# A one-core conv, FFT and FFN kernel: x waits in DRAM for the inverse, the nonlinearity's parts get tiles of their own, ScalarE sums x, and the planner gets margins

## The chip, the cores and the metric

The kernel runs on one core of a Trainium2 chip. The metric is device time in microseconds of one launch. The median of three runs before the change is 4435.95 us (4433.51 to 4437.45). Engine names are those of the profile: PE is TensorE (PEld its weight loads), DVE is VectorE, ACT is ScalarE, POOL is GpSimd, and SP is SyncE, whose queue issues nearly all DMAs.

## The reference, cut to what matters

The input is 32 images of 56 x 56 pixels and 96 channels in float32. Each image passes two layers.

```python
# layer 0: a mixture of 4 experts, weighted per image
pooled = jnp.mean(x, axis=(1, 2));  rw = sigmoid(pooled @ Wr + br)
h = relu(bn1(x @ mix(rw, Wpw) + rw @ bpw))            # 96 -> 384 channels
h = relu(bn2(sum_i rw_i * (depthwise3x3(h, Wdw_i) + bdw_i)))
x = bn3(h @ mix(rw, Wpwl) + rw @ bpwl) + x            # 384 -> 96, "x1" in the kernel
# layer 1, over the image's 3136 tokens t
h = relu(bn(layernorm(t) @ w1.T))                     # 96 -> 192
X = fft(h, tokens)
xr = relu(X.real*rd - X.imag*idg + rb);  xi = relu(X.imag*rd + X.real*idg + ib)
t = t + bn(ifft(xr + 1j*xi).real @ w2.T)
t = t + ffn(layernorm(t))                             # fp8 operands, 96 -> 384 -> 96
```

The pooled mean needs the whole image before the first matrix product of layer 0; the FFT needs all tokens of an image before any frequency, and the inverse needs all frequencies before any token.

## The kernel before, in words

Tokens lie along the free axis and channels on the partitions. x of an image lives in one of three SBUF buffers (`xpad`, line 326); it is loaded there, the projection adds to it in place, the inverse adds to it, the FFN adds to it, and strips of a quarter image are written out from it. So image b can only be loaded when image b-3 is out (`loads`, line 566).

The work of one image is cut into stages, each a Python generator ("stream"). `mixing` (573) sums x on DVE (`pooled`), mixes the expert weights (`wk`, `small`, `wk2`) and copies `wk2` to shifted partitions with six DMAs. `expansion` (643) is the product 96 -> 384 into `ps_pw`, evacuated by ACT to `hp`. The depthwise convolution is split: `convolved_tensor` (678) does four 32-channel blocks at once on PE in three waves of 288 matmul passes (`ps_dw`), and `convolved_vector` (722) does the rest on DVE in steps of one tap. `projection` (748) gives `ps_pwl`, and `projected` (770) adds it to x on DVE. `forward` (814) does layernorm moments by transposes (`ps_t_a`), the product with w1 (`ps_w1`, shown as `ps_w`), the first DFT step (`ps_a`), and sends the result to DRAM (`gd`). `frequency_loads` and `frequencies` bring it back transposed (`g2`), do the second DFT step (`ps_b`), and spawn `nonlinearity` (889) and `spectrum` (934), which does w2 and the first inverse step (`ps_w2`, `ps_c`) and sends `zo` to DRAM (`yd`). `inverse` (979) loads quarter strips `yt`, does the last inverse step (`ps_d`), adds it to x on DVE, transposes again (`ps_t_f`), and runs the FFN (`ps_n`, `ps_f1`, `ps_f2`); POOL casts the hidden values to fp8 and does the last addition before the strip goes out.

The order of all instructions on all engines is written by a planner (`Plan`, 131) when the program is built. It holds a clock per engine, a duration formula per operation (`Engine`, 242, and `mm`, 547), a count of free PSUM tiles (four) and of a few SBUF tiles, and due times of DMAs (`arrives`, 560). `Plan.run` (199) always takes the stream that can start first; ties go by priority. Each engine runs its instructions in exactly that order, and waits at any whose data are not there. Where the planner sees PE wait, `psum` (317) puts in filler matmuls that compute nothing:

```python
for _ in range(min(40, int((plan.idle() - 0.3) / 0.19))):
    nc.tensor.matmul(ps[:PB, 0:PB], dftb_s, dftb_s, start=True, stop=True)
```

They are at line 321 and so can be told from real work (line 554, and 558 for transposes); most other instructions come from line 282.

Of the kernel before, what the change touches and what calls it, by code (L numbers as in the profile page):

```python
# [76 lines left out]
GK = 8  # L77
GROUPS = [(0, 16), (16, 13)]
# [52 lines left out]
class Plan:  # L131
# [9 lines left out]

    def __init__(self, **buffers):
        self.free = dict.fromkeys((PE, DVE, ACT, POOL, SP), 0.0)
        self.now = self.ready = 0.0
        self.events = {}
        self.streams = []

        self.buffers = {tag: [0.0] * n for tag, n in buffers.items()}
        self.busy = dict.fromkeys(self.free, 0.0)

        self.port = {DVE: (0.0, 0.0), POOL: (0.0, 0.0)}

        self.gap = (0.0, 0.0)
# [19 lines left out]
    def release_after(self, n, used):  # L173

        used.append(self.now)
        if len(used) == n:
            self.release(at=max(used))
# [21 lines left out]
    def run(self):  # L199
        while self.streams:  # L200
            best = None
            for stream in self.streams:
                if any(len(self.buffers[tag]) < n for tag, n in stream.takes.items()):
                    continue
                ready = stream.ready
                missing = False
                for key in stream.after:
                    at = self.events.get(key)
                    if at is None:
                        missing = True  # L210
                        break
                    ready = max(ready, at)
                if missing:
                    continue
                for tag, n in stream.takes.items():
                    ready = max(ready, self.buffers[tag][n - 1])
                key = (max(ready, self.free[stream.engine]), stream.priority, ready)
                if best is None or key < best[0]:
                    best = key, ready, stream
            if best is None:  # L220
                raise RuntimeError(
                    "no stream can go on: "
                    + "; ".join(
                        f"{s.name} {[k for k in s.after if k not in self.events]} {s.takes}"
                        for s in self.streams
                    )
                )
            _, ready, stream = best
            has = self.free[PE]
            for tag, n in stream.takes.items():  # L230
                has = max(has, self.buffers[tag][n - 1])
                del self.buffers[tag][:n]
            self.gap = (has, ready) if stream.engine == PE else (0.0, 0.0)
            self.now = self.ready = ready
            self._advance(stream)
# [6 lines left out]
class Engine:  # L242
# [12 lines left out]
    def __getattr__(self, name):  # L255
        def issue(out, *args, **kw):
# [24 lines left out]
            self.plan.tick(self.engine, us, port)  # L281
# [4 lines left out]
def kernel(  # L286
# [39 lines left out]
    xpad = [const([C, (S + 2) * S], F32, f"x_{i}") for i in range(min(3, NB))]  # L326
    xs = [xpad[b % 3][:, S : S + N] for b in range(NB)]
    for b in range(min(3, NB)):
        nc.gpsimd.memset(xpad[b][:, 0:S], 0.0)
        nc.gpsimd.memset(xpad[b][:, S + N :], 0.0)  # L330
# [209 lines left out]
    plan = Plan(ps=4, mir=2, zo=1, h16=4)  # L540
# [19 lines left out]
    def arrives(nbytes, *key):  # L560
        plan.done(*key, late=1.4 + nbytes / 220e3)

    mixed, small_of, wk2s, gds, yds, zs = {}, {}, {}, {}, {}, {}


    def loads():
        for b in range(NB):
            yield SP, [("out", b - 3, s) for s in range(NS) if b >= 3]
            if b:
                Q.dma_start(xs[b], x[b])  # L570
            arrives(4 * C * N if b else 0, "x", b)

    def mixing():

        for b in range(NB):
            yield DVE, [("x", b)] + [("x1", b - 2, s) for s in range(NS) if b >= 2]
            pooled = mixp.tile([C, 1], F32, tag="pooled", name=f"pooled_{b}")
            V.tensor_reduce(pooled, xs[b], AX.X, ALU.add)
            pool_b = mixp.tile([C, 128], F32, tag="pool_b", name=f"pool_b_{b}")
            V.behind.tensor_scalar(pool_b, ones, pooled, 1.0 / N, ALU.mult, ALU.mult)  # L580
# [25 lines left out]
            for c in range(NPE):  # L606
                plan.spawn("diagonals", 3, diagonals(b, c))
# [5 lines left out]
            yield SP  # L613

            wk2s[b] = [wk2]
            for q in range(1, G):
                wk2q = mixp.tile([128, NPE, C], F32, tag=f"wk2_{q}", name=f"wk2_{b}_{q}")
                for to, at in turned(q):
                    Q.dma_start(wk2q[to], wk2[at, 0:NPE])
                wk2s[b].append(wk2q)  # L620
# [22 lines left out]
    def expansion():  # L643

        for b, p, before in parts_of_all():
            xb = xpad[b % 3]
            for c in (2, 0, 1):

                for part, (at, ns) in enumerate((((0, (9, 9)), (18, (8, 8))), ((0, (8, 8)), (16, (9,))))[p]):
                    yield PE, [("wk", b)] + (readers(*before, c) if before else []), 1  # L650
                    wk = mixed[b]
                    ps = psum(f"ps_pw_{b}_{p}_{c}_{part}")
                    for j, n in enumerate(ns):
                        lo = (G * BW * p + at + j * n) * S
                        mm(
                            ps[:, 512 * j : 512 * j + n * S],
                            wk[:, 128 * c : 128 * c + 128],
                            xb[:, lo : lo + n * S],
                        )
                    plan.spawn("evac pw", 5, expanded(b, p, c, part, at, ns, ps))  # L660
# [17 lines left out]
    def convolved_tensor():  # L678

        for b, p, before in parts_of_all():  # L680
            for i, wave in enumerate(WAVES[p]):
# [24 lines left out]
                plan.spawn("evac dw", 0, convolved(b, p, i, wave, ps))  # L706
# [41 lines left out]
    def projection():  # L748

        for b, p, _ in parts_of_all():  # L750
            needs = [("h2t", b, p, i) for i in range(len(WAVES[p]))] + [("wk2", b)]
            needs += [("h2v", b, p, c) for c, *_ in ON_VECTOR[p]]
            for s, blocks in (((0, (0, 1)), (1, (2, 3))), ((2, (4, 5)), (3, (6,))))[p]:
# [13 lines left out]
                plan.spawn("evac prj", 3, projected(b, s, blocks, ps))  # L767
            plan.done("prj", b, p)

    def projected(b, s, blocks, ps):  # L770
# [8 lines left out]
        plan.done("x1", b, s)  # L779

# [33 lines left out]
    def forward(parity):  # L814

        for b in range(NB):
            for s in range(parity, NS, 2):
# [6 lines left out]
                for q0, nq in ((0, 4), (4, 3)):  # L824
                    yield PE, (), 1
                    ps = psum(f"ps_w1_{b}_{s}_{q0}")
                    for q in range(nq):
                        at = s * T + PB * (q0 + q)
                        mm(ps[:PB, 256 * q : 256 * q + CH], xt[:, at : at + PB], w1c)
                    yield DVE  # L830
# [39 lines left out]
    def frequencies():  # L870
# [4 lines left out]
        for b in range(NB):  # L875
            for i, (k0, nk) in enumerate(GROUPS):
                for kind in range(NKIND):
# [6 lines left out]
                    plan.spawn("nonlinearity", 3, nonlinearity(n, b, k0, size, kind, ps))  # L884
                plan.done("g2", n)
                plan.spawn("spectrum", 4, spectrum(n, b, i, k0, nk))
                n += 1

    def nonlinearity(n, b, k0, nk, kind, ps):
        rd, idg, rb, ib = (nl_s[:, j, kind : kind + 1] for j in range(4))  # L890
        nr = nrd[:, kind : kind + 1]
        re = slots(ps, 128, nk, 128, S)
        im = ps[:, 0 : nk * 128].rearrange("p (n w) -> p n w", w=128)[:, :, S:PB]
        yield ACT
        zt = sp.tile([128, GK, PB], F32, tag=f"z_{kind}", name=f"z_{b}_{k0}_{kind}")
        zs[n, kind] = zt
        zr, zi = zt[:, 0:nk, 0:S], zt[:, 0:nk, S:PB]
        A.activation(zi, re, AF.Identity, scale=idg, bias=ib)
        first = k0 == 0 and kind < 2
        if first:  # L900
            A.activation(zr, re, AF.Identity, scale=rd, bias=rb)
            yield DVE
            n0 = CH - 128 if kind else 128
            at0 = zt[:n0, 0, 0 : S + 1 : S]
            V.tensor_add(at0, at0, dc[:n0, kind, :])
        yield ACT, (), "mir"
        used = []
        m = sp.tile([128, GK, PB], F32, tag="mir", name=f"mir_{b}_{k0}_{kind}", bufs=2)
        mr, mi = m[:, 0:nk, 0:S], m[:, 0:nk, S:PB]
        plan.spawn("imaginary parts", 1, imaginary_parts(n, kind, im, zi, mi, rd, nr, used))  # L910
        if not first:
            A.activation(zr, re, AF.Identity, scale=rd, bias=rb)
# [5 lines left out]
        P.tensor_add(mr, mr, zr)  # L918
        yield ACT, [("im", n, kind)]
        A.activation(m[:, 0:nk, :], m[:, 0:nk, :], AF.Relu)  # L920
        yield DVE
        W.scalar_tensor_tensor(zr, zr, 2.0, mr, ALU.mult, ALU.max)
        W.scalar_tensor_tensor(zi, zi, 0.0, mi, ALU.max, ALU.subtract)
        plan.release("mir")
        plan.done("z", n, kind)

    def imaginary_parts(n, kind, im, zi, mi, rd, nr, used):
        yield DVE
        V.scalar_tensor_tensor(mi, im, nr, zi, ALU.mult, ALU.add)
        V.behind.scalar_tensor_tensor(zi, im, rd, zi, ALU.mult, ALU.add)  # L930
        plan.release_after(2, used)
        plan.done("im", n, kind)

    def spectrum(n, b, i, k0, nk):

        for at in range(0, nk, GK):
            some = min(GK, nk - at)
            needs = [("z", n, kind) for kind in range(NKIND)] + [("y", n - 1)] * (n >= 1)
# [40 lines left out]
    def inverse(parity):  # L979


        for b in range(NB):
            for s in range(parity, NS, 2):
                yield SP, [("yd", b, i) for i in range(len(GROUPS))]
# [4 lines left out]
                arrives(4 * PA * SQ * C, "yt", b, s)  # L989
# [6 lines left out]
                strip = xs[b][:, s * T : s * T + T]  # L996
# [8 lines left out]
                yield from moments(f"f_{b}_{s}", xs[b], s, f"f{parity}", got, nt)  # L1005
# [24 lines left out]
                for c in range(NC3):  # L1030
# [8 lines left out]
                    plan.spawn("hidden", 0, hidden(parity, b, s, c, ps, h8))  # L1039
# [22 lines left out]
                arrives(4 * C * T, "out", b, s)  # L1062
# [15 lines left out]
    with tc.manual_schedule():  # L1078
        for name, priority, stream in (
            ("loads", 0, loads()), ("mixing", 5, mixing()), ("inverse", 3, inverse(0)),  # L1080
            ("inverse", 0, inverse(1)), ("frequency loads", 4, frequency_loads()),
            ("frequencies", 3, frequencies()), ("forward", 2, forward(0)),
            ("forward", 1, forward(1)), ("projection", 7, projection()),
            ("vector", 8, convolved_vector()), ("tensor", 6, convolved_tensor()),
            ("expansion", 9, expansion()),
# [117 lines left out]
```

## Time and profile before

| what | value |
|---|---|
| median of three runs | 4435.95 us |
| the profiled execution | 4431.78 us, of which the span is 4429.7 us |
| busy: PE, DVE, ACT, POOL | 97%, 79%, 59%, 22% of the span |
| DMA | 339.19 MB, 16 engines busy 29% in mean |
| DMAs on SP's queue for one image | 41; 10.6 MB is the mean of all images |

The profiled execution was 4.2 us under the median, and 2.1 us of it lie outside the span. A f32 product counts as two matmul passes in the trace. The views used are: the page (busy shares, chain), groups of instructions (count, busy us, mean ns), waits (who waited for whom), the timeline (instructions in order of time, equal ones merged, with the idle time before them), and tables of busy time by stretch.

### The profile page before, as it was taken

The numbers are of one execution on the slowest core, as the hardware profiler recorded it, in microseconds if no ns is written. First come the engines' busy times: TensorE is split into PE (matmuls) and PEld (weight loads), VectorE is DVE, ScalarE is ACT, GpSimd is POOL, SyncE is SP. The second block draws the span as 40 slices with busy tenths as digits, with TensorE's granted clock in tenths as the row PEclk, the third lists the DMA queues.
The fourth block names the chain that finished last, engine by engine and source line by source line (L and its number), as shares of the span: only waits on it lengthen the run. The fifth ranks groups of instructions, "written<-read, shape, count | busy, mean of one in ns | idle before, by whom it ended". The sixth has DMA issues, their size and how long they took to land.

```text
span 4429.7 us, 114914 instructions
## 1 busy us (share of the span) xinstructions
PE 4278.0 (97%) x48916; PEld 3145.0 (71%) x48916; DVE 3503.1 (79%) x7222; ACT 2626.4 (59%) x4135; POOL 979.1 (22%) x1012
## 2 busy tenths in 40 slices
PE   6999999999999999999999999999999999999999
PEld 4767777777777677777677777677777677777778
DVE  6768878888877788877888787888788888788863
ACT  2455666665656655656655666556666656566654
POOL 1012222221222122222122222122222212222222
PEclk9999999999999999999999999999999999999999
DMA  3222233232333222332222332322332322332221
GB/s 92 59 71 63 74 93 81 71 81 67 77 93 80 70 75 71 81 90 74 78 75 71 82 84 72 87 70 71 87 84 71 87 69 67 92 80 71 80 72 50
DMA packets 305448, 339.19 MB, mean 77 GB/s; under 512 B 127908, under 2 KB 244452, under 8 KB 301636
## 3 DMA queue, kind: packets, MB, share of 16 engines
q1 hardware_dynamic: 302824, 331.70, 28.4%
q8 instruction: 384, 6.29, 0.6%
q14 instruction: 128, 1.05, 0.1%
q10 hardware_dynamic: 2112, 0.15, 0.0%
HBM read 164.06 MB, written 158.27 MB: 73 GB/s over the span
## 4 chain that ended last, share of the span: by engine, by line
PE 66%; DVE 15%; ACT 8%; DMA 7%; issue 3%; POOL 1%; SPq 0%; ACTq 0%; POOLq 0%; DVEq 0%
PE ps_dw L554 14%; PE ps_pwl L554 11%; PE ps_w L554 10%; PE ps_pw L554 7%; DVE h L282 6%; PE ps_a L554 5%; PE ps_b L554 4%; PE ps_f L554 4%; DMA x<-in_x_dram 4%; PE ps_c L554 2%; ACT z L282 2%; DMA yd<-zo 2%; DVE z L282 2%; ACT mir L282 2%; DVE pooled L282 2%
## 5 line engine op out<-in xcount | busy, mean ns | idle before, releaser
L282 DVE SCALAR_TENSOR_TENSOR h<-hp,small,h 128x1792 f32<-128x1792 f32 (+2 forms) x768 | 1292.6, 1683 | 33.0 <-ACT h L282 17.3
L554 PE MATMUL ps_dw<-hp,diag 32*32 32x448 f32 x27648 | 857.8, 544 | 9.9 <-issue 9.6
L554 PEld LDWEIGHTS ps_dw<-hp,diag 32*32 32x32 f32 x27648 | 537.9, 103 | 280.6 <-issue 95.8
L282 POOL CAST h<-h 128x784 fp8e5<-128x784 f16 x384 | 382.7, 1022 | 1183.8 <-DVE h L282 1183.8
L554 PE MATMUL ps_pw<-x,wk 96*128 96x448 f32 (+1 forms) x1344 | 572.3, 565 | 38.0 <-DVE z L282 33.8
L554 PE MATMUL ps_pwl<-h,wk 128*96 128x448 f32 x1344 | 526.3, 539 | 0.0
L282 ACT ACTIVATE hp<-ps_pw,small 128x896 f32<-128x896 f32 (+2 forms) x384 | 361.1, 953 | 270.0 <-PE ps_pw L554 256.0
L282 ACT ACTIVATE nt<-yt,nm,rstd_f 112x96 fp8e5<-112x96 f32 x896 | 334.5, 454 | 200.5 <-DVE nm L282 200.3
L554 PEld LDWEIGHTS ps_pw<-x,wk 96*128 96x128 f32 x1344 | 244.4, 190 | 263.4 <-issue 186.4
L282 POOL TENSOR_TENSOR x<-x,y 96x784 f32<-96x784 f32 x128 | 286.8, 2241 | 551.3 <-DVE y L282 528.4
L554 PEld LDWEIGHTS ps_w<-w_s,z 128*112 128x112 f32 (+1 forms) x2816 | 357.3, 179 | 50.7 <-issue 43.2
L282 ACT ACTIVATE h<-ps_dw,small 128x448 f32<-128x448 f32 x384 | 214.8, 630 | 284.2 <-PE ps_dw L554 284.2
L554 PE MATMUL ps_w<-w_s,z 128*112 128x96 f32 (+2 forms) x2816 | 371.7, 286 | 9.6 <-issue 9.1
L554 PEld LDWEIGHTS ps_pwl<-h,wk 128*96 128x96 f32 x1344 | 209.5, 163 | 239.5 <-issue 228.5
L282 DVE SCALAR_TENSOR_TENSOR ha<-ps_w,rstd_a,nshift 112x192 f32<-112x192 f32 x896 | 308.1, 407 | 87.0 <-PE ps_w L554 87.0
L554 PEld LDWEIGHTS ps_b<-dftb_s,g 112*128 112x128 f32 x2816 | 335.1, 192 | 16.2 <-issue 13.2
L554 PE MATMUL ps_w<-w1c,x 96*112 96x192 f32 x1792 | 330.0, 330 | 9.9 <-ACT h L282 7.1
L554 PE MATMUL ps_b<-dftb_s,g 112*128 112x112 f32 x2816 | 339.4, 275 | 0.1
L554 PE MATMUL ps_a<-ha,dfta_s 112*116 112x192 f32 x1792 | 329.2, 329 | 7.7 <-ACT hp L282 7.4
L554 PEld LDWEIGHTS ps_a<-ha,dfta_s 112*116 112x116 f32 x1792 | 285.6, 180 | 36.5 <-ACT hp L282 31.0
L554 PEld LDWEIGHTS ps_w<-w1c,x 96*112 96x112 f32 x1792 | 284.9, 177 | 37.3 <-ACT h L282 18.9
L282 ACT ACTIVATE z<-ps_b,nl_s 128x448 f32<-128x448 f32 (+2 forms) x384 | 248.7, 689 | 89.0 <-PE ps_b L554 88.8
(160 smaller groups left out, 6167.2 us busy)
## 6 DMA issues: line engine op xcount, KB each, us to landing
gd<-g SPq DMA_DIRECT2D x128, 336.0 KB
g<-gd SPq DMA_DIRECT2D x32, 1344.0 KB
x<-in_x_dram SPq DMA_DIRECT2D x32, 1176.0 KB
yt<-yd SPq DMA_DIRECT2D x128, 294.0 KB
out_dram<-x SPq DMA_DIRECT2D x128, 294.0 KB
g<-gd SPq DMA_DIRECT2D x32, 1092.0 KB
gd<-g SPq DMA_DIRECT2D x128, 252.0 KB
yd<-zo SPq DMA_DIRECT2D x96, 336.0 KB
```

The source lines that it names most:

```text
L282: return getattr(self.namespace, name)(out, *args, **kw)
L554: nc.tensor.matmul(to, lhsT, rhs, start=start, stop=stop)
```

## The change

- x gets two SBUF buffers in place of three. After the projection, each strip of x1 is also stored to a DRAM tile (`x1s`, 4 DMAs an image), and the inverse loads it again into a strip tile of its own (four of these, 4 DMAs an image). x of image b is loaded when `forward` has read image b-2 and its x1 is stored; it no longer waits for outputs.
- `pooled` is now an ACT copy of x onto itself with an accumulated sum, not a DVE reduction.
- The nonlinearity keeps `u`, `mr`, `mi` in three tiles (two of each) and not in halves of `z` and `mir`; the Relu of one 128x896 tile becomes two of 128x448, and the imaginary half no longer waits for the real half.
- The six `wk2` copies have one buffer each and wait for the projection of the image before; `pool_b` has one buffer.
- The planner multiplies every duration outside PE by 1.07, takes 2.0 us + bytes/190e3 for a DMA (1.4 + bytes/220e3 before), treats starts up to 0.2 us (PE, ACT) or 0.3 us (DVE) behind an engine's free time as ties, and has other priorities throughout.

No matrix product is added or taken away.

```diff
-    def release_after(self, n, used):
+    def release_after(self, n, used, tag="ps"):
...
-                key = (max(ready, self.free[stream.engine]), stream.priority, ready)
+                at = max(ready, self.free[stream.engine] + self.SLACK[stream.engine])
+                key = (at, stream.priority, ready)
...
-            self.plan.tick(self.engine, us, port)
+            self.plan.tick(self.engine, us * self.plan.MARGIN, port)
...
-    xpad = [const([C, (S + 2) * S], F32, f"x_{i}") for i in range(min(3, NB))]
-    xs = [xpad[b % 3][:, S : S + N] for b in range(NB)]
+    xpad = [const([C, (S + 2) * S], F32, f"x_{i}") for i in range(2)]
+    xs = [xpad[b % 2][:, S : S + N] for b in range(NB)]
...
-        plan.done(*key, late=1.4 + nbytes / 220e3)
+        plan.done(*key, late=2.0 + nbytes / 190e3)
...
-            yield SP, [("out", b - 3, s) for s in range(NS) if b >= 3]
+            yield SP, [(key, b - 2, s) for s in range(NS) for key in ("x read", "x1 by") if b >= 2]
...
-            yield DVE, [("x", b)] + [("x1", b - 2, s) for s in range(NS) if b >= 2]
+            yield ACT, [("x", b)] + [("x1", b - 2, s) for s in range(NS) if b >= 2]
             pooled = mixp.tile([C, 1], F32, tag="pooled", name=f"pooled_{b}")
-            V.tensor_reduce(pooled, xs[b], AX.X, ALU.add)
+            A.activation(xs[b], xs[b], AF.Copy, accum_out=pooled)
...
-            yield SP
+            yield SP, [("prj", b - 1, 1)] * (b >= 1)
...
         plan.done("x1", b, s)
+        yield SP
+        if b not in x1s:
+            x1s[b] = dram.tile([C, N], F32, tag="x1", name=f"x1_{b}", bufs=3)
+        at = slice(blocks[0] * TB, (blocks[-1] + 1) * TB)
+        Q.dma_start(x1s[b][:, at], xs[b][:, at])
+        arrives(4 * C * n * TB, "x1 by", b, s)
...
+        u, mr, mi = (
+            sp.tile([128, GK, S], F32, tag=f"nl{j}", name=f"nl{j}_{b}_{k0}_{kind}", bufs=2)[:, 0:nk]
+            for j in range(3)
+        )
...
-        yield ACT, [("im", n, kind)]
-        A.activation(m[:, 0:nk, :], m[:, 0:nk, :], AF.Relu)
+        yield ACT
+        A.activation(mr, mr, AF.Relu)
         yield DVE
-        W.scalar_tensor_tensor(zr, zr, 2.0, mr, ALU.mult, ALU.max)
-        W.scalar_tensor_tensor(zi, zi, 0.0, mi, ALU.max, ALU.subtract)
...
+        W.scalar_tensor_tensor(zr, u, 2.0, mr, ALU.mult, ALU.max)
...
+        yield ACT
+        A.activation(mi, mi, AF.Relu)
+        yield DVE
+        W.scalar_tensor_tensor(w, w, 0.0, mi, ALU.max, ALU.subtract)
...
-                yield SP, [("yd", b, i) for i in range(len(GROUPS))]
+                yield SP, [("yd", b, i) for i in range(len(GROUPS))] + [("x1 by", b, s) for s in range(NS)], "x1"
+                strip = sp.tile([C, T], F32, tag="x1", name=f"x1_{b}_{s}", bufs=NX1)
+                Q.dma_start(strip, x1s[b][:, s * T : s * T + T])
                 yt = sp.tile([PA, SQ, C], F32, tag=f"yt{parity}", name=f"yt_{b}_{s}")
...
                 Q.dma_start(out[b, :, s * T : s * T + T], strip)
-                arrives(4 * C * T, "out", b, s)
+                plan.release("x1", plan.now + 3.0)
...
-            ("loads", 0, loads()), ("mixing", 5, mixing()), ("inverse", 3, inverse(0)),
-            ("inverse", 0, inverse(1)), ("frequency loads", 4, frequency_loads()),
-            ("frequencies", 3, frequencies()), ("forward", 2, forward(0)),
-            ("forward", 1, forward(1)), ("projection", 7, projection()),
-            ("vector", 8, convolved_vector()), ("tensor", 6, convolved_tensor()),
-            ("expansion", 9, expansion()),
+            ("loads", 1, loads()), ("mixing", 3, mixing()), ("inverse", 6, inverse(0)),
+            ("inverse", 7, inverse(1)), ("frequency loads", 2, frequency_loads()),
+            ("frequencies", 6, frequencies()), ("forward", 6, forward(0)),
+            ("forward", 6, forward(1)), ("projection", 9, projection()),
+            ("vector", 7, convolved_vector()), ("tensor", 4, convolved_tensor()),
+            ("expansion", 10, expansion()),
```

## The prediction

> **What bounds the kernel now.** I read the page first, then the steady part in a table of stretches, then PE's timeline, and last the groups, SP's issues and the waits.
>
> ```profile
> span 4429.7 us, 114914 instructions
> ...
> PE 4278.0 (97%) x48916; PEld 3145.0 (71%) x48916; DVE 3503.1 (79%) x7222; ACT 2626.4 (59%) x4135; POOL 979.1 (22%) x1012
> ...
> PE 66%; DVE 15%; ACT 8%; DMA 7%; issue 3%; POOL 1%; SPq 0%; ACTq 0%; POOLq 0%; DVEq 0%
> ```
>
> PE is busy for 97% of the span and holds 66% of the chain that ended last. But busy is not useful here: the fillers of line 321 count as busy. The built program has 1,383 of them (two passes each).
>
> ```profile
> 2121.93:4127.99 2006.06, 1955.10 (x22502) 1425.68 (x22501) 1636.87 (x3346) 1231.65 (x1935) 458.30 (x465) 1.00 0.30 78
> ```
>
> The first column is the stretch, then its length and PE's busy time. It covers 15 images, from one image's first ps_pw to that of the 15th after: a period of 133.74 us. PE idles 2006.06 - 1955.10 = 50.96 us in it, **3.40 us an image**.
>
> ```profile
> 2068.46 2.62 PE L554 MATMUL ps_pw<-x,wk 96*128 96x448 f32 x6 [1.15 <-DVE z L282]
> ...
> 2114.22 1.80 PE L321 MATMUL ps_w<-dftb_s 112*112 112x112 f32 x16
> 2115.86 2.31 PE L554 MATMUL ps_w<-w_s,z 128*112 128x192 f32 x16
> 2118.01 1.16 PE L321 MATMUL ps_c<-dftb_s 112*112 112x112 f32 x10
> 2119.42 1.08 PE L554 MATMUL ps_c<-zo,dftc_s 112*112 112x384 f32 x4 [0.25 <-ACT zo L282]
> ```
>
> Each row is a start, a length, PE and the group; brackets hold the idle time before it. Sixteen filler passes move the next row from 2114.22 to 2115.86: 1.64 us, 0.1025 a pass, **0.205 us a filler**. The gaps are one of 1.15 us behind a PSUM tile that DVE still reads, and small ones such as 0.25 us.
>
> So PE's time splits: 4278.0 busy less 1,383 x 0.205 = 283.5 of fillers leaves **3994.5 us of real work**, and 4429.7 - 4278.0 = 151.7 us are idle (30.4 of them before PE's first instruction).
>
> [...]
>
> **The change part by part.**
>
> *Order, margins, lifetimes.* Two x buffers, earlier loads of x, separate nonlinearity tiles and new priorities all act through the written order. The built programs say what it becomes: 643 fillers in place of 1,383. In a steady image 29 become 3; start and drain keep theirs (165 to 142 in all up to the third image, 406 to 417 in the last). 740 x 0.205 = **-151.7 us**. That is sure only where PE then finds its data in time, so what is late next decides.
>
> *Round trip of x1.* 256 more DMAs, 2 x 294 KB a strip. SP issues one in 0.32 us: 82 us on a queue that mostly waits. 10.6 MB an image become 13.0, so the mean DMA share goes from 0.30 to about 0.36: hidden on average. It isn't hidden in one burst.
>
> ```profile
> 2101.32 0.32 SPq L282 DMA_DIRECT2D yd<-zo  x1
> 2101.74 1.39 SPq L282 DMA_DIRECT2D x<-in_x_dram  x1
> ```
>
> ```profile
> 2101.74 8.36 DMA x<-in_x_dram
> ...
> 2115.81 2.92 DMA yd<-zo
> ```
>
> The first block is SP's issues, the second the chain: start, length, what. 336 KB alone landed 2.92 us after issue. In the other case 336 + 1176 KB, issued from 2101.32, landed at 2110.10: 8.78 us. So 1204 kB more took 5.86 us, 205 kB/us; x itself landed 8.36 us after its issue.
>
> In the new order of SP this case returns, a 336 KB store of x1 just ahead of the load of x, but with more behind it: four stores of g (522 KB), an output (294), an x1 strip (294), and strip 2 of yt (304.5), 1,414 KB or 1,448 kB. The load of x is released by the last ps_w1 of the image before. PE's work from there to ps_d of strip 2 is, at the timeline's rates: ps_f2 1.00, six ps_a 1.95, ps_n 0.35, six ps_pw 4.72, ps_t_a 0.58, three ps_f1 1.00, four ps_w1 1.30: 10.9 us. The output among them waits for ps_f2 1.0, ACT 0.81, DVE 0.41, POOL 2.24, so it and the strip are issued after about 6 us[...]. x lands at 8.4 + 0.1, and 1,448 kB at 205 to 239 kB/us (the best 4 us stretch beside this x load) later the strip lands: 14.6 to 15.6. **PE waits 3.7 to 4.7 us an image at ps_d, I take 4.2.** The planner does not see this: it prices each DMA alone (5.2 us for the two strips) and puts ps_d at that time. The bounds below and above: 2 us if the engines move at better than 260 kB/us[...]. The load of g2 is next in the ring, 1,376 kB, 7.2 us at the 191 GB/s that such a load showed from 2048 to 2056 us; PE has 6.9 us of work from that ps_d to ps_b. So ps_b waits 0.2 to 0.3 us, I take 0.2.
>
> The other strips are safe by the same count: for strip 0 PE has 19.4 us of work from the last ps_c to ps_d, against DVE's copy of zo 0.66, its store 2.9 and the strip's 3 to 4; strip 3 comes after a 8.7 us wave of ps_dw and more. Strip 1 waits on SP behind the six wk2 copies (3.7 us), which now wait for the projection, and an output: issued some 5 us after ps_pwl and landed 4 to 5 later, against 11.2 us of PE work (ps_dw 8.73, ps_t_a 1.16, ps_d 1.35). So nothing, with 1.5 us to spare.
>
> *Other gaps.* The 1.15 us gap at ps_pw and the wait for pool_b should go with the margins, since real durations outside PE are then under the planned ones. I keep the small ones that the timeline shows four times an image (0.25, 0.23, 0.25, 0.16): 0.9 us. New idle time: 4.2 + 0.2 + 0.9 = 5.3 us an image against 3.40; over the 28 images with 3 fillers **+53.2 us**.
>
> *x summed by ScalarE.*
>
> ```profile
> L282 DVE TENSOR_REDUCE pooled<-x 96x1 f32<-96x3136 f32 x32 | 109.3, 3414 | 28.5 <-DMA x<-in_x_dram 28.5
> L282 ACT ACTIVATE h<-hp,small 128x1792 f32<-128x1792 f32 x32 | 57.3, 1792 | 26.8 <-PE ps_pwl L554 26.5
> L282 ACT ACTIVATE mir<-mir 128x896 f32<-128x896 f32 x96 | 90.9, 947 | 5.5 <-POOL mir L282 5.5
> ...
> L282 ACT ACTIVATE mir<-mir 128x672 f32<-128x672 f32 x32 | 24.4, 764 | 2.3 <-POOL rw L282 1.1 <-POOL mir L282 1.1
> ```
>
> DVE loses 109.3 us. ACT gains 32 x about 3.15 (3136 at 1.0 ns[...]) = 101 us, and 41 us from the split Relu: a line through 896 (947 ns) and 672 (764 ns) gives 581 ns for 448, so each pair costs 0.2 us more. ACT goes from 2626 to some 2770 us, 64% of the new span; nothing on the sum. What queues behind the wait for x on ACT are the evacuations of two ps_pw; PE has tiles free meanwhile because it stands at ps_d. If that cover were gone it would cost up to 3 us an image. *One buffer for wk2's copies and pool_b*: nothing. ps_pwl needs the copies some 30 us of PE work after their release; were that cover gone, their 3.7 us of issue and a landing of some 2 us would stand on PE's path, 5 to 6 us an image. x's earlier load: nothing by itself, since the sum still needs the burst's x at 8.5 us and ACT's 3.2 us, and ps_rw is due only after the delayed ps_d.
>
> ```profile
> PE ps_rw L554 <- DVE pool_b L282: 12.5, 16, 1.6
> PE ps_d L554 <- DMA yt<-yd: 2.3, 3, 1.0
> ```
>
> In the old order PE waited for the mean 12.5 us in all and for yt 2.3: the second is the wait that I expect to grow.
>
> **The sum.** 3994.5 + 643 x 0.205 = 131.8, + 151.7 + 53.2 = 4331.2 us of span; 2.1 outside it, and the median lay 4.2 over the profiled execution: **4337.5 us**, 2.2% less.
>
> **Rivals.** *The plan holds*: the burst is absorbed and 1.2 us an image remain. 3994.5 + 131.8 + 151.7 - 28 x 2.2 = 4216.4, as a median 4222.7. For it: almost no PE wait on a DMA before. Against: the bytes above, which can't be moved in 10.9 us. *Slower*: every strip now needs two tiles; if each of the four fetches is 2.5 us late at ps_d, idle time is 10 + 0.9 us an image, 28 x 7.5 = 210 more than before, 4488 and as a median 4494. It decides from 8.8 us an image on (3.40 + 151.7/28), or 2.0 us a strip. Against it: strips 0 and 3 have slack. *The fillers were free*: their time was waiting anyway and the waits stay, so the same 4436. Against: the new order puts other real work in those places.
>
> **How the numbers follow.** My forecast, with stalls between 2 and 8.5 us and so 4285 to 4427: 0.64. The plan holds or nearly: 0.22. No change: 0.04; slower: 0.10. A measurement here can't tell under 0.2% from nothing. So faster 0.86. The range leaves out the slower case and the best half of the second: 4235 to 4430.
>
> **What would show it.** A steady period near 130 us; line 321 with 1,286 passes; PE's wait ps_d <- DMA (or DVE behind it) at 80 to 150 us in 28 waits and more; DVE busy near 3394, ACT near 2770. I am wrong if ps_d's wait stays under 30 us (then 4220 is near), or if PE waits elsewhere by more than 100 us, at ps_rw or a ps_pw behind ACT's sum first of all.

## The result, and the profile after

The changed kernel takes **4479.1 us** (median of 4 runs, 4472.5 to 4490.5) beside 4435.3 for the kernel before (4433.5 to 4437.5, run with it): a ratio of **1.0101, interval 1.0078 to 1.0124**. It is 1% slower. The forecast was 4337.5 us, in a range of 4235 to 4430; the time lies above all of it. The profiled execution took 4475.08 us.

First the page of the changed kernel: span, busy time of each engine, and the shares of the chain that ended last.

```profile
span 4473.3 us, 112906 instructions
...
PE 4226.8 (94%) x47436; PEld 3048.3 (68%) x47436; DVE 3341.2 (75%) x7254; ACT 2716.2 (61%) x4392; POOL 959.3 (21%) x1010
...
PE 50%; DVE 8%; ACT 7%; DMA 5%; issue 1%; SPq 1%; POOL 0%; POOLq 0%; ACTq 0%; DVEq 0%
```

PE is busy 51 us less than before (4278.0), as fewer fillers would have it, but 740 fillers less are worth 151.7 us, and the real work is the same: 47,436 - 1,286 filler passes here, 48,916 - 2,766 before, 46,150 in both. DVE and ACT fell and rose about as foreseen. PE's share of the chain fell from 66% to 50%. So the time isn't lost to a fuller engine.

Next the steady part, 26 images from one image's first ps_pw to that of the 26th after. The columns are the stretch, its length, busy time of PE, PEld, DVE, ACT and POOL with instruction counts, PE's granted clock, DMA share and GB/s.

```profile
578.04:4097.43 3519.39, 3347.63 (x37649) 2384.57 (x37649) 2699.35 (x5824) 2203.36 (x3562) 777.41 (x806) 0.98 0.35 95
```

And the same 26 images of the kernel before:

```profile
507.73:3986.77 3479.04, 3390.43 (x39000) 2473.43 (x39001) 2837.39 (x5799) 2134.81 (x3355) 793.93 (x806) 1.00 0.30 78
```

The period went from 3479.04 / 26 = 133.81 us to 3519.39 / 26 = 135.36. Times 26 that is 40 of the 44 us by which the two profiled spans differ; what lies outside the 26 images takes 950.7 us before and 953.9 after. The clock column is the new thing: 1.00 before, **0.98** after. Split each period into idle time of PE, filler passes (line 328 in the new file, counted in the timeline, 0.1025 us each) and the rest:

| us an image | period | PE idle | fillers (passes) | rest of PE's busy time |
|---|---|---|---|---|
| before | 133.81 | 3.41 | 5.95 (58) | 124.45 |
| after | 135.36 | 6.61 | 0.62 (6) | 128.13 |
| after, as predicted | 130.4 | 5.3 | 0.62 (6) | 124.45 |

The prediction's row is its idle time and its filler count put on the rest of before. It missed by 5.0 us an image: 1.3 in the idle time, and 3.7 in the rest, which it had held fixed.

**The idle time.** PE's waits in the changed kernel: who waited for whom, us in all, times, longest.

```profile
PE ps_pw L561 <- ACT yt L289: 57.1, 29, 2.0
PE ps_pwl L561 <- DVE z L289: 33.8, 29, 1.2
...
PE ps_c L561 <- ACT zo L289: 23.9, 32, 1.5
PE ps_pw L561 <- ACT g L289: 22.4, 29, 0.8
PE ps_d L561 <- DMA yt<-yd: 21.5, 27, 1.5
PE ps_pw L561 <- DVE z L289: 9.8, 29, 0.3
PE ps_pw L561 <- ACT h L289: 8.3, 30, 0.3
PE ps_d L561 <- ACT h L289: 6.8, 29, 0.2
```

Most rows have 29 waits: the same gap in each image. Six of the eight (yt, z, g, z, h, h) are waits for a **PSUM tile**: ps_pw doesn't read yt or g; ACT's copy of yt is the last reader of the tile that ps_pw is to write. They add up to 138 us. The like rows before are 54 us, these two and ps_w and ps_t_f behind h (7.1 and 5.3):

```profile
PE ps_pw L554 <- DVE z L282: 33.8, 30, 1.4
PE ps_a L554 <- ACT hp L282: 7.4, 29, 0.3
```

That is 84 of the 95 us by which idle time grew (151.7 to 246.5 us). The predicted wait, ps_d behind the DMA of yt, is there, but small.

**The clock.** PE's timeline in two images, around the largest of those waits (start, length, group, idle time before it):

```profile
2246.97 1.93 PE L561 MATMUL ps_pw<-x,wk 96*128 96x504 f32 x4 [0.34 <-DVE z L289]
2250.86 3.20 PE L561 MATMUL ps_pw<-x,wk 96*128 96x448 f32 x4 [1.97 <-ACT yt L289]
...
2791.39 1.93 PE L561 MATMUL ps_pw<-x,wk 96*128 96x504 f32 x4 [0.34 <-DVE z L289]
2795.28 1.77 PE L561 MATMUL ps_pw<-x,wk 96*128 96x448 f32 x4 [1.97 <-ACT yt L289]
```

The wait is 1.97 us in both, the same four matmuls take 3.20 us in one and 1.77 in the other. The trace's record of the granted clock shows what differs. It falls to 0.50 in this run 42 times, each within 0.01 us of a point of one grid with a step of 3.413 us. These are the windows between such points around the two waits (columns as above):

```profile
2247.65:2251.06 3.41, 1.44 (x4) 0.39 (x4) 2.29 (x4) 2.84 (x6) 1.29 (x2) 1.00 0.31 91
2251.06:2254.48 3.42, 3.42 (x6) 1.76 (x6) 3.39 (x15) 2.55 (x4) 0.26 (x2) 0.50 0.02 5
...
2790.37:2793.78 3.41, 2.61 (x12) 1.17 (x10) 3.17 (x5) 2.43 (x5) 2.21 (x2) 1.00 0.30 88
2793.78:2797.20 3.42, 1.92 (x6) 1.16 (x7) 2.51 (x7) 3.39 (x7) 0.90 (x1) 1.00 0.00 0
2797.20:2800.61 3.41, 3.41 (x29) 3.41 (x28) 3.31 (x15) 2.58 (x4) 0.15 (x1) 1.00 0.25 78
```

In the first image the whole wait falls into one window (3.41 - 1.44 = 1.97 us idle), and the granted clock is 0.50 in the next. In the other the same wait lies across a border, 0.80 and 1.50 us, and the clock stays at 1.00. This holds from 500 to 4050 us: of the windows at full clock there, the 35 before a fall hold 1.48 to 1.97 us of idle time, and of the 957 others one holds 1.50 and the rest 1.34 or less. The border between the two in this run, **some 1.5 us idle in one window**, is rough, since the ends of matmuls are modelled, and other runs don't keep to it: in the kernel before one window with 1.90 us kept the clock, and in that kernel without fillers (below) two with 1.5 us or more did, while 5 of its 33 falls follow windows with 1.02 to 1.42 us idle.

Summed over the 26 images, 1 less the clock gives the time lost to it: **80.2 us after, 5.1 before**. It comes in 35 falls, and each costs 1.7 us or 3.4: half of one or two windows, 47 in all. 21 of the 35 (56.3 us) begin at this ps_pw, the other 14 (23.9 us) at the second wait of the list, ps_pwl behind DVE z. PE's timeline there in two images:

```profile
2750.61 1.11 PE L561 MATMUL ps_pw<-x,wk 96*128 96x504 f32 x2 [0.77 <-ACT g L289]
2752.88 6.40 PE L561 MATMUL ps_pwl<-h,wk 128*96 128x448 f32 x12 [1.17 <-DVE z L289]
...
2885.14 1.11 PE L561 MATMUL ps_pw<-x,wk 96*128 96x504 f32 x2 [0.77 <-ACT g L289]
2887.41 4.75 PE L561 MATMUL ps_pwl<-h,wk 128*96 128x448 f32 x12 [1.16 <-DVE z L289]
```

Again the waits are equal and the twelve matmuls are not: 6.40 us or 4.75. No single wait is long here, but 0.77 and 1.17 us stand 1.1 us of work apart, 1.94 us idle in 3.05. In the first image 1.88 us of them fall into one window, in the other they are parted, 0.77 and 1.16, and the clock stays.

So the run is its own experiment: its images have the same waits and differ in the clock. Taken from one ps_pwl to the next:

| windows at half clock in the image | images | mean period, us |
|---|---|---|
| 0 | 1 | 133.5 |
| 1 | 11 | 134.3 |
| 2 | 6 | 135.8 |
| 3 | 8 | 136.7 |

By these sums the clock accounts for (80.2 - 5.1) / 26 = 2.9 of the 3.7 us by which the rest grew. A straight line through the 26 images gives a little less, 1.4 us of the rest for one window and so 2.5 us an image; in the period it is 1.2 us, since PE then waits 0.2 us less. Over the whole span the mean clock, 0.979 against 0.996, gives an estimate of 0.017 x 4473 = 76 us.

What this run shows is thus a clock of 0.50 for one or two steps of 3.413 us, and equal waits with unequal outcomes. No window before a fall was idle throughout: 1.97 us of 3.41 was the most. By what means idle time brings the clock down is not shown.

**Where the 1.97 us come from.** POOL's and ACT's timelines just ahead of it, in this order:

```profile
2243.38 3.47 POOL L289 TENSOR_TENSOR x<-x,y 96x784 f32<-96x784 f32 x1 [0.62 <-DVE y L289]
2246.81 1.35 POOL L289 TENSOR_TENSOR nl<-nl,nl 128x392 f32<-128x392 f32 x1
```

```profile
2248.20 0.53 ACT L289 ACTIVATE nl<-nl 128x392 f32<-128x392 f32 x1 [0.98 <-POOL nl L289]
2248.63 0.61 ACT L289 ACTIVATE z<-ps_b,nl_s 128x336 f32<-128x336 f32 x1
2249.15 1.05 ACT L289 ACTIVATE nl<-ps_b,nl_s 128x336 f32<-128x336 f32 x2
2250.09 0.72 ACT L289 COPY yt<-ps_t_f 112x672 f32<-112x672 f32 x1
```

POOL adds the FFN's output to a strip, and takes 3.47 us here where it takes 1.67 elsewhere in the image (at 2215.31); the planner prices it at 1.9 us times the margin of 1.07. It takes 3.4 us or more where DVE's `h<-hp,small,h` runs beside it: so do all 30 such additions of this trace and all 29 of the trace before, and of the 166 that take under 1.75 us one meets it. The nonlinearity's addition queues behind it on POOL, ACT waits 0.98 us for that, and ACT's copy of yt, ready since PE's transpose ended at 2246.6, comes four instructions later in ACT's order, at 2250.09. Its end frees the PSUM tile, and PE goes on at 2250.86. So POOL holds PE up for about 1 of the 1.97 us; the rest are ACT's own four instructions. No filler stands here, because the planner counts from the time at which it believes PE and the tile to be free to the time at which the data are there: a wait for the tile itself never gets one.

### The profile page after: what moved, and what is told of

Read it like the earlier page. It is cut to its first block, busy times and chain, and to the rows that moved or that the text cites. A ratio compares the mean times of both kernels' runs of the same rounds, so it can differ in the third digit from the quotient of the medians.

```text
span 4473.3 us, 112906 instructions
## 1 busy us (share of the span) xinstructions
PE 4226.8 (94%) x47436; PEld 3048.3 (68%) x47436; DVE 3341.2 (75%) x7254; ACT 2716.2 (61%) x4392; POOL 959.3 (21%) x1010
## 4 chain that ended last, share of the span: by engine, by line
PE 50%; DVE 8%; ACT 7%; DMA 5%; issue 1%; SPq 1%; POOL 0%; POOLq 0%; ACTq 0%; DVEq 0%
PE ps_dw L561 10%; PE ps_w L561 9%; PE ps_pwl L561 9%; PE ps_pw L561 5%; PE ps_a L561 4%; PE ps_b L561 3%; DVE h L289 3%; PE ps_c L561 3%; PE ps_f L561 2%; DMA yt<-yd 2%; ACT nl L289 2%; PE ps_d L561 2%; ACT h L289 2%; DVE z L289 1%; DMA g<-gd 1%
## 5 line engine op out<-in xcount | busy, mean ns | idle before, releaser
L289 DVE SCALAR_TENSOR_TENSOR h<-hp,small,h 128x1792 f32<-128x1792 f32 (+2 forms) x768 | 1254.2, 1633 | 56.0 <-ACT h L289 42.0
L289 POOL CAST h<-h 128x784 fp8e5<-128x784 f16 x384 | 395.1, 1047 | 1723.8 <-DVE h L289 1715.9
L561 PE MATMUL ps_pw<-x,wk 96*128 96x448 f32 (+1 forms) x1344 | 627.4, 594 | 97.5 <-ACT yt L289 57.1
L561 PE MATMUL ps_pwl<-h,wk 128*96 128x448 f32 x1344 | 552.9, 561 | 33.8 <-DVE z L289 33.8
L561 PEld LDWEIGHTS ps_pwl<-h,wk 128*96 128x96 f32 x1344 | 224.6, 169 | 326.7 <-issue 264.9
L289 POOL TENSOR_TENSOR x<-x,y 96x784 f32<-96x784 f32 x128 | 269.7, 2107 | 553.2 <-DVE y L289 387.3
L561 PEld LDWEIGHTS ps_w<-w_s,z 128*112 128x112 f32 (+1 forms) x2816 | 366.4, 183 | 29.8 <-DVE h L289 15.4
L289 DVE SCALAR_TENSOR_TENSOR x<-ps_pwl,small,x 96x896 f32<-96x896 f32 (+1 forms) x128 | 131.9, 1030 | 292.9 <-PE ps_pwl L561 292.9
L561 PE MATMUL ps_a<-ha,dfta_s 112*116 112x192 f32 x1792 | 349.6, 341 | 0.0
L289 ACT CAST h<-ps_f 128x784 f16<-128x784 f32 x384 | 292.9, 820 | 82.8 <-PE ps_f L561 79.2
L561 PEld LDWEIGHTS ps_a<-ha,dfta_s 112*116 112x116 f32 x1792 | 309.3, 190 | 27.6 <-issue 12.6
```

The source lines that it names most:

```text
L289: return getattr(self.namespace, name)(out, *args, **kw)
L561: nc.tensor.matmul(to, lhsT, rhs, start=start, stop=stop)
```

## The experiments

Ratios are to the kernel before, each run beside it on its chip.

**More fillers at the wait.** If the clock is the loss, eight fillers before the one ps_pw that precedes the wait should *shorten* the run, though they add work.

```
-            for _ in range(min(40, int((plan.idle() - 0.3) / 0.19))):
+            more = 8 if name.endswith("_0_2_0") and name.startswith("ps_pw_") else 0
+            for _ in range(min(40, max(more, int((plan.idle() - 0.3) / 0.19)))):
```

> The changed kernel with at least 8 fillers ahead of the first ps_pw of every image, just before the place where PE waits some 2 us for a PSUM tile and the granted clock falls in the trace; nothing else differs. Theory (the clock): about 5.7 us an image at half clock cost some 80 us in all, and these fillers stand where PE idles anyway, so the clock rises from 0.979 to 0.99 or more and the time falls from 4479 to 4390-4425 us. Rival (waits alone, the clock is a side effect without weight): no change within 10 us, or up to 248 x 0.205 = 51 us more.

Measured: 4414.0 us (4412.4 to 4417.7), ratio 0.9954 [0.9939, 0.9968], clock 0.994. From its page, its waits and its PE timeline:

```profile
span 4415.9 us, 113898 instructions
...
PE 4212.0 (95%) x47932; PEld 3047.6 (69%) x47932; DVE 3338.3 (76%) x7254; ACT 2716.5 (62%) x4392; POOL 958.4 (22%) x1010
```

```profile
PE ps_pw L562 <- ACT yt L289: 11.4, 29, 0.4
```

```profile
2226.32 1.80 PE L329 MATMUL ps_pw<-dftb_s 112*112 112x112 f32 x16 [0.33 <-DVE z L289]
2227.95 1.87 PE L562 MATMUL ps_pw<-x,wk 96*128 96x504 f32 x4
2230.22 1.77 PE L562 MATMUL ps_pw<-x,wk 96*128 96x448 f32 x4 [0.40 <-ACT yt L289]
```

496 matmuls more than the changed kernel, and PE is busy *less*: 4212.0 us against 4226.8. In a steady image fillers grew by 16 passes, 1.64 us, and idle time fell by 1.46, which nearly cancels; the gain is in the rest, 2.3 us (128.13 to 125.79). All 29 rows that follow the wait now take 1.77 us. The clock theory holds, and the gain is 65 us by the medians. Of the falls 8 remain, 13.7 us; 7 of them are at ps_pwl, which this edit doesn't touch, and one at a ps_c that waits 1.32 us for ACT's zo.

**Half of them**, `more = 4`:

> The changed kernel with 4 fillers in place of 8 ahead of each image's first ps_pw. Theory (what matters is that PE does not stand near 2 us at one stroke): the wait shrinks to about 1.2 us, as long as waits that leave the clock alone in both kernels, so clock 0.99 or more and 4400-4425 us. Rival (the whole wait must be filled, or the fillers act by their number): between the two, 4440-4470.

Measured: 4416.4 us (4407.9 to 4422.6), 0.9957 [0.9942, 0.9973], clock 0.997. The wait is 34.2 us in all, 1.18 each, and in the profiled execution no fall begins there: 1.18 us in this place leave the clock alone, where 1.97 us did not; the least idle time of a window before a fall in the changed kernel was 1.48. The 5 falls that remain are at ps_pwl.

**The same fillers in another ps_pw**, as a control (`name.endswith("_1_2_0")` in the first edit):

> Control to the run with more fillers: the same 8 fillers an image, but ahead of the first ps_pw of an image's second half, where the trace of the changed kernel shows no wait on a PSUM tile. Theory (the clock falls at one place, behind one 2 us wait): they only displace real work there and the clock stays near 0.979, so 248 x 0.205 = 51 us more, or 20-50 if some fall into small waits: 4500-4530. Rival (any added PE work keeps the clock up): 4410-4430 as with the fillers at the other place.

Measured: 4480.3 us (4469.8 to 4484.2), 1.0083 [1.0054, 1.0113], clock 0.981. Its waits:

```profile
PE ps_pw L562 <- ACT yt L289: 57.1, 29, 2.0
...
PE ps_d L562 <- DMA yt<-yd: 2.7, 3, 1.4
```

The same count of fillers, in the wrong place, doesn't move the time: the 1.97 us wait and the low clock stay. Falls still cost 64.8 us in the 26 images. I had expected the fillers to cost time, 20 us or more. They don't: PE waits at ps_d for yt a little later and that wait shrinks from 21.5 to 2.7 us, so of 1.64 us of fillers an image 0.8 come out of idle time; another 0.6 are fewer windows at half clock (64.8 us lost in place of 80.2).

**The strip addition on POOL left out**, its place in the order kept:

```
-                P.tensor_add(strip, strip, y16)
+                plan.tick(POOL, (0.1 + T * 2.3 / 1000.0) * plan.MARGIN, True)
```

> The changed kernel without POOL's last addition of the FFN output to the strip (that term is missing from the output); the planner still books its time, so every order stays. Theory (ACT stands in order behind POOL's nl, which stands behind this addition): PE's wait ps_pw <- ACT yt falls from 57 us to under 20, the clock event behind it goes, 4479 becomes 4365-4400. Rival (ACT is late by its own load): that wait stays at 40 us or more and the time changes by less than 15 us.

Measured: 4376.2 us (4372.7 to 4380.6), 0.9868 [0.9853, 0.9882], clock 0.993. The wait behind yt falls to 25.5 us in all, 0.88 each, which is not under 20 as expected: POOL's part of it is gone and ACT's own is left. No row right after it is slow, and the period is 132.3. Part of this gain is work that is simply missing, so the next run counts more.

**The addition moved behind the nonlinearity**, all work done:

```
         P.tensor_add(mr, mr, u)
+        plan.done("pn", n, kind)
...
-                yield POOL
+                yield POOL, [("pn", 2 * b + 3, 2)] * (s == 2 and 2 <= b < NB - 1)
```

> The changed kernel with one wait added in the planner: strip 2's last addition on POOL comes after the three nl additions of the second frequency group, not between them; all work is done. Theory (ACT stands behind POOL's nl, that behind the addition): ps_pw <- ACT yt falls from 57 us to under 30, clock 0.99, time 4375-4420 us, below the kernel before's 4436. Rival (the wait moves: the later output holds SP's queue and what is issued behind it): 4460-4490.

Measured: 4416.9 us (4410.2 to 4422.0), 0.9950 [0.9933, 0.9966], clock 0.995. The timeline of PE in it, and the addition's group in POOL's list (busy time, mean ns):

```profile
2226.36 1.93 PE L561 MATMUL ps_pw<-x,wk 96*128 96x504 f32 x4 [0.33 <-DVE z L289]
2229.18 1.77 PE L561 MATMUL ps_pw<-x,wk 96*128 96x448 f32 x4 [0.89 <-ACT yt L289]
```

```profile
L289 POOL TENSOR_TENSOR x<-x,y 96x784 f32<-96x784 f32 x128 | 219.5, 1714 | 528.6 <-DVE y L289 362.8 <-PE ps_pwl L561 108.6 <-issue 57.2
```

The wait is 0.88 to 0.89 us in 27 images and 1.97 in the first two. Falls cost 15.4 us in the 26 images, all at ps_pwl. With one step moved and nothing taken out, 62 us come back. The edit isn't quite alone: the planner's new order has 20 filler passes in a steady image where the changed kernel has 6. That these are not the cure is argued from two runs above: in one, 16 passes in another place did nothing for the wait; in the other it fell to 0.88 us with the old 6 passes. The addition itself went from a mean of 2107 ns to 1714: it no longer runs beside DVE's `h<-hp,small,h` but in 4 of 128 times.

**Both cures at once**, the moved addition and the eight fillers:

> The same as the run with POOL's addition later, with the 8 fillers ahead of each image's first ps_pw as well. Theory (both act on one wait): they do not add up; once the wait is short the fillers displace work, so equal to the better of the two alone or up to 40 us worse: 4390-4440. Rival (independent causes): 65 us and 60-100 us add up, 4320-4350.

Measured: 4428.0 us (4416.2 to 4436.6), 0.9972 [0.9959, 0.9986], clock 0.997. They don't add up: they cure the same thing, and the fillers (36 passes an image) are then more than the waits can hold.

**Fillers also at the second largest wait**, ps_pwl behind DVE z (33.8 us): the first edit, and four before the ps_pw ahead of it.

```
+            if name.endswith("_1_1_1") and name.startswith("ps_pw_"):
+                more = 4
```

> The changed kernel with the 8 fillers of the first run and 4 more in the tile just ahead of the second ps_pwl, which waits 1.17 us an image for a PSUM tile that DVE still reads. Theory (PE's waits for PSUM tiles get no fillers from the planner but are waits all the same): the wait shrinks by some 0.8 us, the fillers cost nothing, 4414 within 10 us. Rival (more PE work is more time): 28 x 0.82 = 23 us more, 4430-4445.

Measured: **4406.3 us** (4398.9 to 4410.3), **0.9930 [0.9908, 0.9952]**, clock 0.999: the fastest that does all the work, ahead of both kernels. Its waits:

```profile
PE ps_pw L564 <- ACT yt L289: 11.4, 29, 0.4
PE ps_pwl L564 <- DVE z L289: 10.9, 29, 0.4
```

Idle time falls by another 0.8 us an image and fillers grow by the same; the rest falls by 0.5, which is what the 13.7 us of falls were in the run before it. In the 26 images of the profiled execution (clock 0.999; 0.997 to 0.998 in the other three) there is **no fall at all**: with the two waits nearly the whole loss of clock is gone.

**The kernel before without any filler** (`for _ in range(0)`). It tests the prediction's first step, that a filler is 0.205 us of PE's time for nothing.

> The kernel before with all 1,383 fillers left out, order and real work the same. Theory (the clock): PE idles 6 us more an image in a few stretches of 2-4 us, the clock falls below 0.985 and the time rises by 60 to 120 us to 4495-4555. Rival (fillers displace real work): the time falls, by up to 283 us. Rival (fillers are free and useless): 4436 within 10 us, clock unchanged.

Measured: 4465.7 us (4460.3 to 4469.8), 1.0068 [1.0053, 1.0083], clock 0.963. Its page, and its first wait:

```profile
span 4460.6 us, 109384 instructions
...
PE 4144.8 (93%) x46150; PEld 2939.6 (66%) x46150; DVE 3504.4 (79%) x7222; ACT 2626.4 (59%) x4135; POOL 978.9 (22%) x1012
```

```profile
PE ps_c L554 <- ACT zo L282: 106.7, 66, 2.9
```

283.5 us of fillers taken out; idle time rises from 151.7 to 315.8 us, and PE's other work from 3994.5 to 4144.8, the same matmuls. The sum is +31. The direction was expected, the size is half of the lowest that was. The mean clock alone, 0.963 against 0.996, gives an estimate of 0.033 x 4460.6 = 147 us of the 150; it is too high by what falls into idle time. In 26 steady images the falls take 87 us more than before, and PE's other work grows by 94. So the fillers of before were not a cost that an order could simply save: over half of their time was waiting in any case, and the rest bought the clock.

**The sum on ACT made short**: 56 columns of x in place of 3136, the order kept.

> The changed kernel with ScalarE's sum of x over 56 columns in place of 3136 (the pooled mean is then wrong), orders kept. Theory (the sum is covered): within 15 us of 4479, since PE hardly waits for the evacuations behind it. Rival (the 3.1 us block of ACT costs PE each image): 40 to 90 us less.

Measured: 4472.7 us (4468.8 to 4475.1), 1.0085 [1.0068, 1.0102], clock 0.977. ACT is busy 78 us less (2637.8) and the time stays near that of the changed kernel; the intervals overlap. The sum on ACT is covered, as the prediction had it.

**The halves of the change.** The new data flow with the old priorities, margin and DMA prices:

> The changed kernel's data flow (x1 through DRAM, separate nonlinearity tiles, sum by ScalarE) with the planner of before: no margin, no slack, old DMA times and priorities. Its order has 1,033 fillers, 17.5 an image. Theory (the data flow is sound, the loss lies in an order whose waits the planner didn't see): clock 0.985 or more, 4390-4445. Rival (the data flow itself costs: more DMA, more ACT operations): 4480 or more whatever the planner.

Measured: 4698.9 us (4687.5 to 4703.6), 1.0580 [1.0553, 1.0607]. My theory of this run fell. The period alternates between about 132 and 155 us: every second image is as short as in the best runs and the others have a hole. That is an order that doesn't fit the new waits, and no proof that the data flow is slow in itself: with another order and a few fillers the same data flow takes 4406 us (above). What makes the hole was not followed up.

The new data flow and priorities with no margins (`MARGIN = 1.0`, slacks 0, a DMA at 1.4 us + bytes/220e3 in place of 2.0 + bytes/190e3):

> The changed kernel, priorities too, but the planner without margin and slack and with the DMA times of before; its order has 800 fillers, 19 and 3 in turn. Theory (an order planned on durations that are too short meets waits it did not foresee): 4500 or more. Rival (margins only lengthen the plan): 4440-4480 or less.

Measured: 4496.3 us (4494.4 to 4501.1), 1.0136 [1.0115, 1.0158], clock 0.979. That is just under the 4500 that the theory gave as its least. Periods alternate here too, with a mean of about 137 us, and the largest wait is PE's ps_d behind ACT's g, 60.5 us in 13 waits up to 5.7.

The old data flow with the new priorities, margins and prices:

> The kernel before with the planner's margin, slack, DMA times and priorities of the changed kernel, its data flow as it was. The order has 3,095 fillers. Theory (an order's priorities fit one data flow only; x in three buffers and outputs ahead of loads hold this one up): 4650 or more. Rival (the new planner is the better one for any data flow): under 4435.

Measured: 4887.1 us (4876.2 to 4892.5), 1.1013 [1.0986, 1.1039]. Periods go from 101 to 203 us, with 3,095 fillers. Alone, one half costs 261 us and the other 451, each beside its own runs of the kernel before; together they cost 44. Neither has a price of its own, so the loss of the change can't be shared out between them.

## Why the prediction was wrong

**The step that failed is the first of the sum: "740 x 0.205 = -151.7 us", with "3994.5 us of real work" held fixed under it.** The filler count was right (643, three in a steady image), and so is 0.205 us each. What it was taken to mean was wrong, in three ways.

- *PE's other time isn't a constant.* It rose by 100.5 us over the whole run (4226.8 - 643 x 0.205 = 4095.0), for the same 46,150 passes. Of the 3.7 us in a steady image, some 2.5 to 2.9 are a clock that falls after two waits: shown by the images of one run, by fillers added at those places and elsewhere, and by the moved addition. The text expected PE to idle more, and priced an idle microsecond at one microsecond.
- *The filler count doesn't measure PE's waiting.* A filler stands where the planner sees data late; in the new order most of the waiting is for PSUM tiles (138 of 246.5 us), which gets none. Few fillers were read as little waiting. The caveat, "sure only where PE then finds its data in time", named data and not the place to put the result.
- *Fillers were work that paid.* Taking them all out of the kernel before costs 31 us. The rival "the fillers were free", at 4436, was nearer; it had "the waits stay" and lacked the clock.

**"Other gaps: 0.9 us"** failed with it. The step let the gap at ps_pw go "with the margins, since real durations outside PE are then under the planned ones". One isn't: POOL's addition, 3.47 us against 1.9 x 1.07 = 2.0 planned. The trace of before already had it, with a mean over the planned time and 29 of 128 at 3.4 us or more:

```profile
L282 POOL TENSOR_TENSOR x<-x,y 96x784 f32<-96x784 f32 x128 | 286.8, 2241 | 551.3 <-DVE y L282 528.4 <-PE ps_a L554 17.7 <-ACT rstd_f L282 3.2
```

Gaps behind PSUM tiles are 138/29 = 4.8 us an image, and ps_c behind zo is 0.75 more (23.9 us in 32 waits). The text's own last sentence named the place, "a ps_pw behind ACT", but behind ACT's sum; it is behind ACT's copy, held up by POOL.

**"PE waits 3.7 to 4.7 us an image at ps_d, I take 4.2"** had the right place and releaser and five times the size: 21.5 us in 27 waits and 2.6 at ps_b, 0.8 us an image. The mis-sized term is the DMA rate. A stretch of the changed kernel, SP's issues in it, and the ps_d that waits:

```profile
2182.50:2193.00 10.50, 10.22 (x54) 6.92 (x53) 4.50 (x19) 8.85 (x11) 4.54 (x7) 1.00 0.94 277
```

```profile
2182.09 0.32 SPq L289 DMA_DIRECT2D x<-in_x_dram  x1
2184.78 1.68 SPq L289 DMA_DIRECT2D gd<-g  x4
2186.55 0.33 SPq L289 DMA_DIRECT2D out_dram<-x  x1
2186.93 0.96 SPq L289 DMA_DIRECT2D x<-x  x1
2187.94 2.49 SPq L289 DMA_DIRECT2D yt<-yd  x2
```

```profile
2193.96 1.55 PE L561 MATMUL ps_d<-dftd_s,yt 116*96 116x112 f32 x14 [0.41 <-DMA yt<-yd]
```

The burst is as drawn: x, four stores of g, an output, an x1 strip and yt behind it, with the engines 94% busy. But they move 277 GB/s, not the 205 to 239 taken from before, where two landings and one mixed stretch gave the rate (the trace of before has 253 in the 4 us from 2103). yt is in use 11.9 us after x's issue, not 14.6 to 15.6 and more. The text's lower bound, 2 us at better than 260, was still too high. The bytes and PE's work were right, and the rate taken was 14 to 26% too low. That the strip lands after all that was issued ahead of it was the author's estimate, and is not shown. That the idle time as a whole came within 1.3 us of the forecast is luck: 3.6 us too much at ps_d and ps_b stand against 4.9 too little elsewhere.

**What held.** ACT's and DVE's load (2716 and 3341 us against 2770 and 3394; x's sum takes 2818 ns a piece, under the 3.15 us taken: 1.0 ns an element was a whole duration, 1792 ns for 1792 elements, and the text's own line through 896 and 672 elements, 947 and 764 ns, gives an estimate of 0.82 ns an element, a fixed 0.21 us, and so 2.78 us), the sum covered on ACT, x1's trip through DRAM covered on average (share 0.35 against 0.36), start and drain unchanged, strips 0, 1 and 3 in time. One sum doesn't come out, without weight for the outcome: "stalls between 2 and 8.5 us and so 4285 to 4427". 8.5 us of idle time give 4427, but 2 us give 4245, and 4276 if only ps_d's wait is 2.

**What stays open.** With no fall of the clock left PE's rest is still 125.3 us an image, 1.0 over before's 124.45 less 0.2 of its own falls. Small waits that end inside a matmul's modelled time would look like this; that is argued, not shown. It is shown beside which instruction of DVE POOL's addition is slow, and not why. Nor was an order tried from a planner that knows POOL's 3.47 us.

## What to carry to other kernels

Don't take "busy less fillers" for work: it depends on the clock, and here 1.48 to 1.97 us of waiting within one window of 3.41 us were followed by 1.7 or 3.4 us of lost clock, so price where the waits lie and not only their sum. Ask of every wait of PE if it is for data or for a PSUM tile, and follow a tile's wait back through the order of each engine's instructions to the first instruction that runs longer than planned. When a planner's count of gaps falls, first see which gaps it counts.

## What was not expected of the hardware

- In the changed kernel the granted clock fell to 0.50 for one or two windows of a grid with a step of 3.413 us, after each of 35 windows with 1.48 to 1.97 us of idle PE, and after none of 957 others with at most 1.50. In 26 images there were 21 falls at a wait of 1.97 us, and 14 at waits of 0.77 and 1.17 us with 1.1 us of work between, by where they stood on the grid; with the first wait at 1.18 us (half the fillers) none began there. With eight fillers in place one fall came at a wait of 1.32 us, at ps_c.
- Matmuls that compute nothing made the run shorter: 16 passes an image, -65 us.
- POOL's addition of 96x784 took 1.67 us, or 3.47 beside DVE's `h<-hp,small,h`.
- Loads and stores in a mixed burst moved 277 GB/s for 10.5 us; the estimate from two landings had been 205.
